# Graph network kernel: ranks counted by partition, uneven transfers issued in two, and the second convolution's table built inside the first convolution's loop

## The chip, the cores and the metric

The kernel runs on one NeuronCore of a Trainium2 chip. The metric is the device time of one execution, in microseconds (us). The core has five engines with an instruction stream each: TensorE (PE, matrix products, with weight loads shown as PEld), VectorE (DVE), ScalarE (ACT), GpSimd (POOL) and SyncE (SP, which here only issues transfers). Transfers between HBM and the on-chip memory (SBUF) are issued by SP, ACT or POOL, each from its own instruction stream, and are done by 16 DMA engines. Matrix products land in PSUM, which has eight banks.

## The reference: what is computed

A graph of N = 6250 nodes with 128 features each and E = 100000 edges, sorted by destination. Two layers, each followed by a layer norm over the features:

```python
edge_index = stack([src, dst])
x = layernorm(x + sigmoid(gcn(relu(gcn(x, W1, b1)), W2, b2)))      # layer 0: two graph convolutions
x = layernorm(x + attention(x, edge_attr, fc_w, fc_r_w, attn_w, loop_w, src, dst))   # layer 1

# one graph convolution; a loop of weight 1 is added to every node
deg  = segment_sum(ew, dst)
dinv = rsqrt(deg)
out  = segment_sum((x @ W)[src] * (dinv[src] * ew * dinv[dst])[:, None], dst) + b
# layer 1: scores from z[src], z[dst] and the edge attributes, a softmax over the edges of
# each destination, and a sum of alpha * (z[src] + edge_attr @ fc_r_w.T) by destination
```

All is float32. The edge attributes are E x 128 floats, 51 MB, and are read twice.

## The kernel before, in words

**Chunks.** The edges are cut into NC = 49 chunks of 2048 (16 per partition); the last chunk has 1696, so 106 partitions of 16. The edges being sorted by destination, a chunk's destinations lie in a window of WC = 144 consecutive nodes whose start is read at run time (`cbase_of`). Nodes are cut into NB = 49 blocks of 128; the last block has 106 nodes.

**Sorting (L688 to L787).** In each chunk the edges are ordered by the block of their source. For every edge the kernel finds its rank, the number of earlier edges of its chunk with the same source block. A comparison makes a one-hot tile `oh` of 128 partitions x 48 blocks x 16 edges (L698). VectorE adds it up over 2, 4 and 8 edges (L703 to L705), and ten TensorE products (L710 to L714) fill a tile of two PSUM banks with, for each edge position and block, the number of earlier edges. ScalarE copies that tile out (L717), and VectorE multiplies it with `oh` and adds it up over the blocks (L718 to L723). When all chunks of a batch (seven, at first three and four) have ranks, each edge gets a slot: 12 groups of 128 slots, in which each quarter takes edges of one source block, and GS = 5 groups for edges that spill. Further one-hot tiles and products move each edge's source row, window position and weight to its slot (L757 to L773). The source rows of a batch go to HBM (`srd`, L781).

**One convolution (`pick`, `weigh`, `scatter`, `add_in`, L467 to L527).** The table, one row for each node, lies in HBM (`g1`, `g2`) and, its first 48 blocks split into three bf16 parts, in SBUF (`hot`). For a chunk, `pick` multiplies a mask of the slots (a comparison of the slot's source row with the partition, L853) with `hot` on TensorE (144 products, L476); ScalarE copies the result out with the edge weights (L481); POOL gathers the spilled edges' rows from HBM (L485); VectorE makes the window positions one-hot (L491, L498). `scatter` sums the 17 groups into the window on TensorE (L522), `add_in` adds the window to the accumulator on VectorE (L527).

**The stages.** Preparation and the node degrees (to about 115 us). The table of the first convolution (`table_of`, L324): for each four blocks four products with W1, a scaled copy, a store to `g1`, the split into `hot`, and a transpose into the accumulator `acc1`, which so starts with the node's own term. The first convolution's loop (L862), in which the sorting of the later chunks is interleaved: it is done when seven chunks are left. Then all of `acc1` is scaled by dinv (L308) and goes through bias and ReLU (L885), and `table_of` builds the second table from it, into `g2`, `hot` and a second accumulator `acc2`. The second convolution's loop (L999) loads the masks back from HBM, and in it VectorE also multiplies the edge attributes by the attention vector and adds them up (L980, L981); in steps of four blocks, nodes that are done go on to the first layer's result and the table of the second layer (`x1_of` under `Pieces`: `go` takes up a group of blocks once the running window has passed it). That table goes to HBM (`zd`, and split in `hz`); the attention stage (L1028 on) loads `hot` again from `hz` in four slices on ACT's queue (L1191), computes the scores (L1053 to L1097) and the softmax in batches, and runs the last loop.

**What sets the order.** Each engine runs its instructions in program order. The order is fixed at build time by a planner that goes through the program with a cost model and takes what is ready, in the order of the program where several are; it inserts the semaphore waits and gives tiles a place as their buffers come free. The second convolution's loop is kept as written (`manual_schedule`). The first convolution's loop is not. A pool's `bufs` says how many buffers a tile has in turn.

**Lines of the prediction's steps.** L308 scaling by dinv, L320 to L322 the split of a table (its last subtraction on POOL), L423 to L425 the same split in `x1_of`, L333 and L340 products and transposes of `table_of`, L334 and L342 ScalarE's copies in it, L421 to L426 the parts' store, L827 the load of the degrees, L849 and L854 the load of slot rows and the store of masks, L994 the load of edge attributes, L1106 the load of one batch's scores.

## Time and profile before

| | |
|---|---|
| median of 8 executions | 1987.57 us (1983.59 to 1993.39) |
| the profiled execution | 1987.97 us; its span, first to last instruction, 1986.2 us |
| mean granted TensorE clock in it | 0.90 of full speed |
| TensorE / VectorE / ScalarE / POOL busy | 80% / 82% / 48% / 56% of the span |
| first convolution's loop | about 170 to 678 us |
| second table | about 678 to 735 us |
| second convolution's loop | about 735 to 1194 us |
| attention stage | about 1194 to 1986 us |
| moved by DMA | 307 MB, 155 GB/s over the span |

In the profile L12 is line 12 of the kernel before; an arrow `out<-in` names the tile written and those read. In a list in order of time a line gives the start, the duration, the engine and the operation, and in square brackets how long the engine sat idle before it and what ended that. `DMA_DIRECT2D` on SPq or ACTq is the issue of a transfer, not its duration. In a list of waits the columns are the total, the number of times and the longest, in us.

### The profile page before, as it was taken

Reading aid. Unit: us, or ns where it says so; the run is one execution under the profiler, and the core shown is the slowest. Engines: PE = TensorE matmul, PEld = TensorE weight load, DVE = VectorE, ACT = ScalarE, POOL = GpSimd, SP = SyncE. Lnnn points to the kernel's source line nnn. Section 1 sums busy time; section 2 is a strip of 40 time slices with the busy share of each in tenths; the row PEclk is TensorE's granted clock in tenths of the full one; section 3 lists DMA queues with packets and bytes.
Section 4 is the critical chain, followed back from the end, with each engine's and each line's share of the span. In section 5 each row is a group of like instructions: output and inputs, shape, how many; then the busy total and the mean of one; then the engine's idle time right before and its main releaser. Section 6 shows DMA issues by size and latency. Waiting matters only on the chain.

```text
span 1986.2 us, 78720 instructions
## 1 busy us (share of the span) xinstructions
PE 1591.2 (80%) x33767; PEld 1439.9 (72%) x33767; DVE 1633.0 (82%) x3252; ACT 945.8 (48%) x3098; POOL 1107.1 (56%) x953
## 2 busy tenths in 40 slices
PE   2867889989987868888888884568888888888996
PEld 2556878878877757778778872457777777877985
DVE  7788978888977338998989965889989898997773
ACT  1255445455455655667667663113343343434543
POOL 4025766676676548888888860215344343434762
PEclk9978989999988959899989995569899999999998
DMA  2114244244245337777767774636656666655662
GB/s 63 37 44 151 68 117 132 48 144 138 64 124 179 76 120 222 236 228 226 253 219 237 243 230 131 180 106 173 181 159 191 169 179 179 180 165 144 191 184 68
DMA packets 254593, 306.90 MB, mean 155 GB/s; under 512 B 37857, under 2 KB 193255, under 8 KB 247182
## 3 DMA queue, kind: packets, MB, share of 16 engines
q1 hardware_dynamic: 222627, 244.90, 39.1%
q0 software_dynamic: 23520, 48.22, 11.8%
q10 hardware_dynamic: 8088, 8.65, 1.4%
q8 instruction: 268, 4.39, 0.9%
q14 instruction: 90, 0.74, 0.1%
HBM read 260.42 MB, written 41.25 MB: 152 GB/s over the span
## 4 chain that ended last, share of the span: by engine, by line
PE 38%; DVE 35%; DMA 13%; issue 7%; ACT 5%; POOL 1%; DVEq 1%; SPq 0%; ACTq 0%; POOLq 0%
PE win L522 16%; PE g L476 8%; DVE wm L491 5%; DMA far<-g,sidx 4%; DVE sel L1096 3%; DVE put L764 3%; DVE ohm L759 2%; PE rec L1209 2%; DMA rk<-srow 2%; DMA mask<-srd 2%; DMA mask<-masks 2%; PE mm L333 1%; PE k L1093 1%; ACT got L481 1%; PE r L1239 1%
## 5 line engine op out<-in xcount | busy, mean ns | idle before, releaser
L485 POOL DMA_INDIRECT far<-g,sidx x490 | 728.3, 1486 | 231.2 <-PE win L522 94.6
L481 ACT ACTIVATE got<-g,swt 128x128 f32<-128x128 f32 x1764 | 485.9, 381 | 390.2 <-PE g L476 188.1
L485 POOL DMA_INDIRECT far<-zd,sidx x245 | 314.1, 1282 | 451.2 <-PE win L522 330.5
L522 PE MATMUL win<-wm,got 128*128 128x144 f32 x3528 | 524.1, 306 | 11.8 <-issue 11.7
L522 PEld LDWEIGHTS win<-wm,got 128*128 128x128 f32 x3528 | 487.0, 204 | 30.2 <-issue 20.8
L476 PE MATMUL g<-hot,mask 128*32 128x128 bf16 x21168 | 395.2, 230 | 84.7 <-issue 61.4
L476 PEld LDWEIGHTS <-mask 128*32 128x32 bf16 x21168 | 338.8, 102 | 118.9 <-issue 89.6
L491 DVE TENSOR_TENSOR wm<-iota,sdst 128x1728 f32<-128x1728 f32 x147 | 286.8, 1951 | 4.5 <-DMA g<-rows 4.3
L515 ACT ACTIVATE wm<-wm,swt 128x64 f32<-128x64 f32 (+1 forms) x735 | 201.1, 355 | 78.2 <-DVE wm L498 46.4
L522 PE MATMUL win<-wm,far 128*128 128x64 f32 (+1 forms) x1470 | 187.6, 272 | 24.6 <-DMA far<-g,sidx 22.3
L522 PEld LDWEIGHTS win<-wm,far 128*128 128x128 f32 x1470 | 181.9, 194 | 26.6 <-issue 21.4
L527 DVE TENSOR_TENSOR acc<-acc,win 128x144 f32 x147 | 44.4, 302 | 104.2 <-PE win L522 92.1
L1093 PE MATMUL k<-adp,rk 128*128 128x49 bf16 x2352 | 90.6, 193 | 48.9 <-DVE sel L1096 35.3
L980 DVE TENSOR_TENSOR et<-et,ar_row 128x2048 f32<-128x2048 f32 (+1 forms) x49 | 111.6, 2278 | 20.1 <-DMA et<-in_edge_attr_dram 20.1
L1093 PEld LDWEIGHTS <-rk 128*128 128x128 bf16 x2352 | 83.0, 102 | 60.3 <-issue 30.8
L981 DVE TENSOR_REDUCE dots<-et 128x16 f32<-128x2048 f32 (+1 forms) x49 | 112.0, 2286 | 1.7
L322 POOL TENSOR_TENSOR hot<-low,hot 128x512 bf16<-128x512 f32 x24 | 32.5, 1356 | 138.5 <-DVE hot L321 99.2
L1096 DVE TENSOR_TENSOR sel<-k,ohb 128x392 f32<-128x392 f32 x98 | 83.7, 854 | 2.6 <-PE k L1093 2.0
L764 DVE TENSOR_TENSOR put<-ohg,rec 128x1360 bf16<-128x1360 bf16 x49 | 76.9, 1569 | 0.0
L717 ACT CAST own<-r 128x768 bf16<-128x768 f32 x49 | 39.3, 801 | 71.4 <-PE r L714 49.8
L771 PE MATMUL rec<-put,ohm 128*128 128x90 bf16 x784 | 59.7, 244 | 14.8 <-DVE put L767 12.7
L771 PEld LDWEIGHTS <-ohm 128*128 128x128 bf16 x784 | 55.5, 165 | 20.8 <-DVE put L767 10.2
(397 smaller groups left out, 2308.8 us busy)
## 6 DMA issues: line engine op xcount, KB each, us to landing
et<-in_edge_attr_dram SPq DMA_DIRECT2D x97, 512.0 KB
et<-in_edge_attr_dram SPq DMA_DIRECT2D x48, 1024.0 KB
mask<-masks SPq DMA_DIRECT2D x98, 384.0 KB
rk<-srow SPq DMA_DIRECT2D x98, 256.0 KB
mask<-srd SPq DMA_DIRECT2D x49, 384.0 KB
masks<-mask SPq DMA_DIRECT2D x49, 384.0 KB
far<-g,sidx POOLq DMA_INDIRECT x490
g<-rows SPq DMA_DIRECT2D x24, 256.0 KB
```

Of the source, the lines that this page charges most:

```text
L476: nc.tensor.matmul(ps[32 * q : 32 * q + 32, g, :], mask[:, (g0 + g) * P + 32 * q : (g0 + g) * P + 32 * q + 32], hot[:, 4 * (g0 + g) + q, k ...
L481: nc.scalar.activation(got[:, g, :], ps[:, g, :], AF.Copy, scale=swt[:, c, g0 + g : g0 + g + 1])
L485: nc.gpsimd.indirect_dma_start(out=got, out_offset=None, in_=table[:, :], in_offset=bass.IndirectOffsetOnAxis(ap=sidx[:, c, g : g + 1], ax ...
L491: nc.vector.tensor_tensor(wm[:, : GP * WC].rearrange("p (g w) -> p g w", w=WC), iota[:, None, 1 : WC + 1].to_broadcast([P, GP, WC]), sdst[ ...
L515: nc.scalar.activation(m, m, AF.Copy, scale=swt[:, c, g : g + 1])
L522: nc.tensor.matmul(ps[:, n0 : n0 + m.shape[-1]], rows[g], m, start=g == 0, stop=g == G - 1)
L764: nc.vector.tensor_tensor(put[:, :, : G * F].rearrange("p t (g f) -> p t g f", f=F), ohg[:, :, :, None].to_broadcast([P, TC, G, F]), rec[: ...
L771: nc.tensor.matmul(ps, ohm[:, :, t], put[:, t, :], start=t == 0, stop=t == TC - 1)
L980: nc.vector.tensor_mul(et[:n], et[:n], ar_row[:n, None, :].to_broadcast([n, TC, D]))
L981: nc.vector.tensor_reduce(dots[:n, c, :], et[:n], AX.X, OP.add)
L1093: nc.tensor.matmul(ps[:, s, :], mk[:, s * P : (s + 1) * P], adp[:, 0, k, :NB], start=k == 0, stop=k == 2)
L1096: nc.vector.tensor_mul(sel, ps, ohb.rearrange("p b s -> p s b"))
```

## The change

Four edits, in one step.

1. *Ranks by partition.* The rank of an edge may count the edges of its chunk in any fixed order. Now the partitions are ordered by a spread number (partition x 79 mod 128, `first`), and inside a partition the order of the 16 edges holds. The edges of earlier partitions are counted by sixteen TensorE products of 48 columns that add up in one tile of one PSUM bank, of which there are two; ScalarE copies that tile out, repeated 16 times. The edges of the same partition are counted on VectorE: a 16 x 16 comparison of the source blocks, a product with a lower triangle, a reduction into `near`, which is added once a batch. The additions L703 to L705 and the ten products L710 to L714 go.
2. *Uneven transfers in two.* `even(n)` cuts a transfer over n partitions into one over the largest multiple of 16 and one over the rest. It is used for the last block of nodes (106: 96 and 10), the last chunk's edge attributes (106), the degrees (49: 48 and 1) and the scores of a batch (34, 82 or 114).
3. *The second table in the first loop.* `h_of` takes a group of four blocks of `acc1`, once the window has passed it, through scaling, bias, ReLU, the product with W2, the store to `g2`, the transpose back into `acc1` and the split into three bf16 parts, which go to HBM (`hh`). Two steps of it are called in each turn of the loop; what is left runs after the loop. `hot` is then loaded from `hh` in four slices on ACT's queue. The tile of the rows (`hrows`) and that of the parts (`hpart`) have one buffer, and the first subtraction of the split writes in place into `hrows`. To make room in PSUM the window tile of this loop has one bank in place of two.
4. *One tile for both sums.* `acc2` is `acc1`.

```diff
+    spread = const.tile([P, P + 1], I32, name="spread")
+    for of, at in ((iota_i[:, :P], slice(0, P)), (iotap_i[:, 0:1], slice(P, P + 1))):
+        nc.vector.tensor_scalar(spread[:, at], of, 79, None, op0=OP.mult)
+        nc.vector.tensor_scalar(spread[:, at], spread[:, at], P - 1, None, op0=OP.bitwise_and)
+    spread_f = const.tile([P, P + 1], F32, name="spread_f")
+    nc.vector.tensor_copy(spread_f, spread)
+    first = const.tile([P, P], BF16, name="first")
+    nc.vector.tensor_scalar(first, spread_f[:, :P], spread_f[:, P:], None, op0=OP.is_gt)
+    lower = const.tile([P, TC, TC], BF16, name="lower")
+    nc.vector.tensor_tensor(lower, iotab[:, None, :TC].to_broadcast([P, TC, TC]),
+                            iotab[:, :TC, None].to_broadcast([P, TC, TC]), op=OP.is_lt)
...
+    def even(n):
+        cut = n // 16 * 16
+        return [slice(a, b) for a, b in ((0, cut), (cut, n)) if b > a]
...
         if b1_ == NB:
-            eng.dma_start(table[(NB - 1) * P : N, :], of[:tail, NB - 1 - b0, :])
+            for r in even(tail):
+                eng.dma_start(table[(NB - 1) * P + r.start : (NB - 1) * P + r.stop, :], of[r, NB - 1 - b0, :])
...
+    def h_of(acc, b0, n, xp, pool):
+        some = blocks[b0 : b0 + n]
+        w = sum(nb for _, nb in some)
+        at = slice(b0 * P, b0 * P + w)
+        scale = by_dinv(acc, b0, n, xp)
+        next(scale)
+        yield
+        next(scale, None)
+        yield
+        nc.scalar.activation(acc[:, at], acc[:, at], AF.Relu, bias=cols[:, 0:1])
+        yield
+        st = xp.tile([P, 4, D], F32, name="hrows", bufs=1)
+        ps = pool.tile([P, 4, D], F32, name="mm")
+        for b, nb in some:
+            nc.tensor.matmul(ps[:nb, b - b0, :], acc[:, b * P : b * P + nb], w2, start=True, stop=True)
+            nc.scalar.activation(st[:nb, b - b0, :], ps[:nb, b - b0, :], AF.Copy, scale=dinv[:nb, b : b + 1])
+        store_blocks(nc.sync, g2, st, b0, n)
+        yield
+        ps = pool.tile([P, 512], F32, name="mm")
+        for b, nb in some:
+            nc.tensor.transpose(ps[:, (b - b0) * P : (b - b0) * P + nb], st[:nb, b - b0, :], ident[:nb, :nb])
+        nc.scalar.copy(acc[:, at], ps[:, :w])
+        if b0 < BP:
+            m = min(n, BP - b0)
+            part = xp.tile([P, 4, 3, D], BF16, name="hpart", bufs=1)
+            nc.scalar.copy(part[:, :m, 0, :], st[:, :m])
+            yield
+            left = st[:, :m]
+            nc.vector.tensor_sub(left, left, part[:, :m, 0, :])
+            nc.vector.tensor_copy(part[:, :m, 1, :], left)
+            nc.vector.tensor_sub(part[:, :m, 2, :], left, part[:, :m, 1, :])
+            nc.sync.dma_start(hh[:, b0 : b0 + m], part[:, :m])
...
-    ps_r = sorting.enter_context(tc.tile_pool(name="ps_r", bufs=1, space=PSUM))
+    ps_r = sorting.enter_context(tc.tile_pool(name="ps_r", bufs=2, space=PSUM))
...
-                a2 = sp.tile([P, BP, 8], BF16, name="a2")
-                a4 = sp.tile([P, BP, 4], BF16, name="a4")
-                a8 = sp.tile([P, BP, 1], BF16, name="a8")
-                nc.vector.tensor_tensor(a2, oh[:, :, 0:8], oh[:, :, 8:16], op=OP.add)
-                nc.vector.tensor_tensor(a4, a2[:, :, 0:4], a2[:, :, 4:8], op=OP.add)
-                nc.vector.tensor_tensor(a8, a4[:, :, 0:1], a4[:, :, 2:3], op=OP.add)
-                ps = ps_r.tile([P, 2, 512], F32, name="r")
-                for h in range(2):
-                    ks = slice(h * HB, h * HB + HB)
-                    full = ps[:, h, : HB * TC].rearrange("p (k t) -> p k t", t=TC)
-                    nc.tensor.matmul(full, trib, oh[:, ks, :], start=True, stop=False)
-                    nc.tensor.matmul(full[:, :, 8:16], onesb, oh[:, ks, 0:8], start=False, stop=False)
-                    for of, m, w in ((a2, 2, 4), (a4, 4, 2), (a8, 8, 1)):
-                        to = full.rearrange("p k (b i) -> p k b i", b=m)[:, :, :, w : 2 * w]
-                        nc.tensor.matmul(to, onesb, of[:, ks, None, 0:w].to_broadcast([P, HB, m, w]),
-                                         start=False, stop=w == 1)
+                ps = ps_r.tile([P, BP], F32, name="r")
+                for t in range(TC):
+                    nc.tensor.matmul(ps, first, oh[:, :, t], start=t == 0, stop=t == TC - 1)
+                pairs = sp.tile([P, TC, TC], BF16, name="pairs", bufs=1)
+                nc.vector.tensor_tensor(pairs, blk[:, c, :, None].to_broadcast([P, TC, TC]),
+                                        blk[:, c, None, :].to_broadcast([P, TC, TC]), op=OP.is_equal)
+                nc.vector.tensor_mul(pairs, pairs, lower)
+                nc.vector.tensor_reduce(near[:, c - c0, :], pairs, AX.X, OP.add)
                 own = sp.tile([P, BP, TC], BF16, name="own", bufs=2)
-                nc.scalar.copy(own.rearrange("p (h k) t -> p h (k t)", h=2), ps[:, :, : HB * TC])
+                nc.scalar.copy(own, ps[:, :, None].to_broadcast([P, BP, TC]))
...
+            nc.vector.tensor_add(r_, r_, near[:, :n])
...
-            ps_w = ... tile_pool(name="ps_w", bufs=2, space=PSUM)
+            ps_w = ... tile_pool(name="ps_w", bufs=1, space=PSUM), ps_m = ... tile_pool(name="ps_m", bufs=1, space=PSUM)
...
+        pieces = Pieces(lambda b0, n: h_of(acc1, b0, n, hp, ps_m))
...
             if win is not None:
                 add_in(acc1, c - 2, win)
+            pieces.go(lows[max(c - 1, 0)], 1)
             new = pick(c, mask, hot, g1, ps_g, wp, 6, 12)
             sort_to(to)
+            pieces.go(lows[max(c - 1, 0)], 1)
             slot_rows(c + 2)
...
         add_in(acc1, NC - 1, scatter(held, ps_w))
+        pieces.go(N, 999)
+        for b0 in range(0, BP, GP):
+            nc.scalar.dma_start(hot[:, b0 : b0 + GP], hh[:, b0 : b0 + GP])
...
-    with tc.tile_pool(name="rows1", bufs=4) as xp:
-        scaled(acc1, xp)
-    for c, n in chunks512:
-        nc.scalar.activation(acc1[:, c : c + n], acc1[:, c : c + n], AF.Relu, bias=cols[:, 0:1])
-    leftB = ctx.enter_context(ExitStack())
-    acc2 = leftB.enter_context(tc.tile_pool(name="accp2", bufs=1)).tile([P, NP], F32, name="acc2")
-    with tc.tile_pool(name="tab2", bufs=2) as wp, tc.tile_pool(name="ps_t", bufs=3, space=PSUM) as ps_mm:
-        table_of(acc1, w2, g2, hot, acc2, ps_mm, wp)
+    acc2 = acc1
...
-                nc.sync.dma_start(ets[c][:n], ea[c * CC : c * CC + n * TC, :].rearrange("(p t) f -> p t f", t=TC))
+                of = ea[c * CC : c * CC + n * TC, :].rearrange("(p t) f -> p t f", t=TC)
+                for r in even(n):
+                    nc.sync.dma_start(ets[c][r], of[r])
```

The loads of a last block (`load_some`), of the degrees (L827) and of the scores (L1106) are cut by `even` in the same way.

More of the change, by code (lines that the diff above doesn't have):

```diff
@@ L76, in gnn_kernel @@
     BP = 4 * GP
-    HB = BP // 2
     G = GP + GS
@@ L109, in gnn_kernel @@
     hz = dram.tile([P, BP, 3, D], BF16, name="hz")
+    hh = dram.tile([P, BP, 3, D], BF16, name="hh")
     dinvd = dram.tile([NB, P], F32, name="dinvd")
@@ L264, in load_some @@
         if b0 + n >= NB:
-            eng.dma_start(to[:tail, NB - 1 - b0, :], of[(NB - 1) * P : N, :])
+            for r in even(tail):
+                eng.dma_start(to[r, NB - 1 - b0, :], of[(NB - 1) * P + r.start : (NB - 1) * P + r.stop, :])
     def transpose_blocks(pool, to, of, first=0, count=NB):
@@ L692, in sort @@
             some = slice(c0, c0 + n)
+            near = sp.tile([P, BATCH, TC], F32, name="near", bufs=1)
             rank = sp.tile([P, BATCH, TC], F32, name="rank")
@@ L826, in gnn_kernel @@
             degr = xp.tile([NB, 3, P], F32, name="degr")
-            nc.sync.dma_start(degr, degd.rearrange("k b p -> b k p"))
+            for r in even(NB):
+                nc.sync.dma_start(degr[r], degd.rearrange("k b p -> b k p")[r])
             nc.vector.tensor_add(degr[:, 0, :], degr[:, 0, :], degr[:, 1, :])
@@ L837, in gnn_kernel @@
         table_of(xT, w1, g1, hot, acc1, ps_mm, xp, lambda: sort_to(min(done[0] + 1, steps_to(sorts[1][0]))))
-    with tc.tile_pool(name="conv", bufs=2) as wp, tc.tile_pool(name="ps_g", bufs=3, space=PSUM) as ps_g, \
-            tc.tile_pool(name="ps_w", bufs=2, space=PSUM) as ps_w:
+    with tc.tile_pool(name="conv", bufs=2) as wp, tc.tile_pool(name="hp", bufs=2) as hp, \
+            tc.tile_pool(name="ps_g", bufs=3, space=PSUM) as ps_g, \
+            tc.tile_pool(name="ps_w", bufs=1, space=PSUM) as ps_w, tc.tile_pool(name="ps_m", bufs=1, space=PSUM) as ps_m:
         rows_in = {}
@@ L879, in gnn_kernel @@
         add_in(acc1, NC - 1, scatter(held, ps_w))
+        pieces.go(N, 999)
+        for b0 in range(0, BP, GP):
+            nc.scalar.dma_start(hot[:, b0 : b0 + GP], hh[:, b0 : b0 + GP])
     sorting.close()
     edges.close()
-    with tc.tile_pool(name="rows1", bufs=4) as xp:
-        scaled(acc1, xp)
-    for c, n in chunks512:
-        nc.scalar.activation(acc1[:, c : c + n], acc1[:, c : c + n], AF.Relu, bias=cols[:, 0:1])
-    leftB = ctx.enter_context(ExitStack())
-    acc2 = leftB.enter_context(tc.tile_pool(name="accp2", bufs=1)).tile([P, NP], F32, name="acc2")
-    with tc.tile_pool(name="tab2", bufs=2) as wp, tc.tile_pool(name="ps_t", bufs=3, space=PSUM) as ps_mm:
-        table_of(acc1, w2, g2, hot, acc2, ps_mm, wp)
-    rightA.close()
+    acc2 = acc1
     with tc.tile_pool(name="conv2", bufs=2) as wp, tc.tile_pool(name="arp", bufs=2) as ap_, \
@@ L1105, in softmax @@
             ad = lp.tile([P, P], F32, name="ad", bufs=1)
-            nc.sync.dma_start(ad[:R, :], adgd[c0 * CC : c0 * CC + R * P].rearrange("(r j) -> r j", j=P))
+            rows = adgd[c0 * CC : c0 * CC + R * P].rearrange("(r j) -> r j", j=P)
+            for r in even(R):
+                nc.sync.dma_start(ad[r, :], rows[r, :])
             ps = ps_c.tile([P, P], F32, name="rec")
@@ L1290, in gnn_kernel @@
     right_r.close()
-    leftB.close()
+    rightA.close()
     hotp.close()
```

## The prediction

> **What bounds the kernel now.** First the page's shares and slices, to see whether one engine bounds the whole.
>
> ```profile
> PE 1591.2 (80%) x33767; PEld 1439.9 (72%) x33767; DVE 1633.0 (82%) x3252; ACT 945.8 (48%) x3098; POOL 1107.1 (56%) x953
> DVE  7788978888977338998989965889989898997773
> ```
>
> VectorE and TensorE share the lead, but the two 3s in VectorE's slices (680 to 740 us) are a stage in which neither works much. So the stages come next, as stretches of the first convolution's loop and what follows it (columns: stretch, length, busy time of PE, PEld, DVE, ACT, POOL, granted clock, DMA share, GB/s).
>
> ```profile
> 320.00:400.00 80.00, 70.99 (x1492) 64.69 (x1494) 70.71 (x157) 41.34 (x143) 56.09 (x38) 0.94 0.40 116
> 400.00:480.00 80.00, 69.13 (x1640) 62.08 (x1632) 73.34 (x161) 44.20 (x152) 56.26 (x41) 0.98 0.45 130
> 640.00:680.00 40.00, 37.01 (x804) 35.61 (x804) 17.14 (x29) 25.58 (x88) 23.51 (x20) 0.96 0.44 105
> 680.00:740.00 60.00, 41.44 (x314) 30.49 (x317) 18.12 (x28) 31.93 (x85) 20.10 (x16) 0.60 0.33 107
> ```
>
> While edges are sorted, VectorE is busy 88 to 92% and bounds the loop; after the last sort (from about 625 us) TensorE does. 680:740 is the second table, a chain of TensorE and ScalarE at a clock of 0.60. Then the waits of the loop, 170 to 640 us (us in total, times, longest):
>
> ```profile
> DVE own L718 <- ACT own L717: 20.0, 13, 2.9
> DVE mask L853 <- DMA mask<-srd: 17.0, 11, 6.6
> ...
> SPq L781 <- DVE srT L780: 248.9, 6, 44.8
> ```
>
> VectorE was busy 400 of these 470 us. The third line matters later: SyncE's queue stands still for half of the loop, behind a store that waits for the end of each sorted batch. Last, in order of time, the two edges between loops.
>
> ```profile
> 678.46 0.30 DVE L527 TENSOR_TENSOR acc<-acc,win 128x144 f32 x1 [4.59 <-PE win L522]
> 732.46 0.42 SPq L994 DMA_DIRECT2D et<-in_edge_attr_dram  x1
> 735.44 5.27 PE L476 MATMUL g<-hot,mask 128*32 128x128 bf16 x197 [7.59 <-DMA mask<-masks]
> 737.67 2.29 DVE L980 TENSOR_TENSOR et<-et,ar_row 128x2048 f32<-128x2048 f32 x1 [3.13 <-DMA et<-in_edge_attr_dram]
> 744.66 4.42 PE L522 MATMUL win<-wm,got 128*128 128x144 f32 x24
> ...
> 1165.34 0.26 SPq L994 DMA_DIRECT2D et<-in_edge_attr_dram  x1
> 1196.83 2.29 DVE L980 TENSOR_TENSOR et<-et,ar_row 106x2048 f32<-106x2048 f32 x1 [16.93 <-DMA et<-in_edge_attr_dram]
> 1233.53 0.32 SPq L426 DMA_DIRECT2D hz<-part  x1
> 1236.19 0.33 ACTq L1191 DMA_DIRECT2D hot<-hz  x1
> 1247.56 1.15 PE L476 MATMUL g<-hot,mask 128*32 128x128 bf16 x36
> ```
>
> From the last addition of the first convolution to the first window sum of the second, 678.5 to 744.7, 66 us pass. At the second edge VectorE idles 16.9 us for one load: 848 KB in 106 partitions, 31.5 us from issue to use, where the 1 MB load of 128 partitions at 732.46 took 5.2.
>
> **The ranks.** Per chunk three additions go (L703, L704, L705: 353, 253 and 201 ns in the loop, 807 in all) and three operations come. The comparison of 128x256 resembles L761 (272 elements, one operand repeated innermost, 438 ns): 415. The product of 256 packed bf16 lies between L704 (192, 253) and L703 (384, 353): 286. The reduction of 256 resembles L1097 (392 elements, 555 ns) by length: 416. Sum 1117, so +0.31 us a chunk on VectorE; 42 chunks are sorted in the loop, 13 us, and six batch additions at 270 ns (L742) make 1.6. TensorE's ten matmuls of 192 to 384 columns take 1.2 us a chunk (403.01 to 404.2); sixteen of 48 columns resemble L1209 (51 columns, sixteen in 1.12 us): 0. The moving operand now has a stride of 32 bytes, which no row shows for a moving operand; as weights such a stride loads in 165 ns (L771) against 102 (L1093), so at most +1 us a chunk on TensorE, in the phase where VectorE binds: taken as 0. ScalarE's copy keeps 768 elements (801 ns): 0. Two rank banks in place of one take away part of the 20.0 us that VectorE waits for that copy.
>
> **The second table's work, moved into the loop.** Per piece of four blocks VectorE gets the scaling (L308, 687 ns), two subtractions (L423 681, L425 696, the second one formerly on POOL as L322, 1356 ns) and a cast (L321, 456): 2.52 us. Nine pieces lie in the sorting part: 22.7 us. ScalarE gets 0.735 + 4 x 0.369 + 0.586 + 0.699 = 3.5 us a piece, in a loop where it is busy 52%: hidden by that slack; without it 9 x 3.5 = 31. TensorE: 49 blocks took 41.4 us at a clock of 0.60, so about 2 us a piece at full clock; nine are 18 us, in its 60 idle us of this stretch: hidden while VectorE binds. SyncE carries per piece one row load, one g2 store and now one store to hh (0.35 us of issue each), between the mask stores. VectorE's sum is 13 + 1.6 + 22.7 = 37, less 0.08 us overlap of back-to-back instructions (two of L698 in 1.01 us at 0.55 each), 35. Bounds for the loop: 0 (all of it goes into the 70 us of idle time) and 35/0.88 = 40. I take 26: 35 less about half of the 20 us on the copy, the wait that the second bank bears on.
>
> **The wait added.** The first subtraction writes in place into the tile that the g2 store reads, so VectorE waits for that store; behind it stand masks and sort work, and TensorE's next pick. A store-to-load step takes 2.66 us (1233.53 to 1236.19). From 0 (half a chunk, 5 us, lies between) to 9 x (2.66 + 4.31, a mask-store pair at 412.12 on SyncE) = 63. The nearest row is the mask load, late 11 times in 48 by 1.5 us: 2 or 3 waits of 2 us, +5. The window bank is single now: scatter waits for the addition before it, which starts 0.2 us after its window ends (416.28), 4 us ahead of the next scatter; when it falls behind L491 and L498, 2.4 us, in the seven unsorted chunks 17: +1.
>
> **Edge 1.** Gone are 66 us. New: the last chunk's gathers meet three 1152 KB slices of hot, as those at 1182.84 did (10.63 us in the chain against 4.89 at 673.02): +5. After the last addition, the last piece: scaling 0.40, ReLU 0.49, TensorE 0.7, copies 0.75, store landed 2.66, VectorE 0.8, hh landed 2.66 (rows of the piece at 1224 to 1236): 8.5. Then the fourth slice; its like was used 11.4 us after issue behind other work, and 5.2 us is a free 1 MB load: 8. The rest of pick 0 and pick 1: 3. Together 24.5, gain 42. Ends: -50 (no contention, 5 us slice) and -24 (all 4.6 MB and two 1 MB loads only after the last piece: 6.6 MB at the 240 GB/s of 1000 to 1100 us is 28, with 8.5 and 5, 42). Between, because slices at 1177.64 to 1185.94 went out as the last pick freed them. The piece before shares the single tiles, but starts 5 us earlier (673.56): 0. POOL's gathers wait for g2's last store, 3 us before hh's: 0. On ScalarE's queue the fourth load waits for hh; behind it stand the evictions of pick 0, which need that slice anyway: 0.
>
> **Uneven transfers.** If the 848 KB land like the 1 MB load, VectorE's 16.9 us go, but the second loop's last gathers (10.63) and the rk load behind them (8.09) are late next, still beside the hot slices. 0 to -17; I take -7, half of both. The other splits (1 KB to 53 KB) cost an issue of 0.3 us each; the one wait seen is 0.71 us, the ad load of 3.37 stands once in the chain: -1 (ends -4, +1; the row sum of the degrees used 10 us after issue was not waited for).
>
> [...]
>
> **Before the loop.** Seven chunks at 0.31 us: +2 (ends 0, +5 with the new constants, 1.7 us, whose cover is a 2.59 us wait at 6.5 us).
>
> **Sum.** The profiled execution took 1987.97 us (span 1986.2, 1.8 around it), 0.4 above the median of eight, 1987.57. 26 + 5 + 1 - 42 - 7 - 1 + 2 = -16: 1972.
>
> **Rivals.** *The in-place wait decides (slower).* Place: the subtraction behind g2's store. For: SyncE blocked up to 44.8 us at a time. Against: a store that is ready earlier is queued earlier. Full price 63 instead of 5: 2030; slower begins where each of nine pieces waits 2.8 us (16 + 4 + 5 over 9). *The loop swallows the work.* For: 70 us idle, the second rank bank. Against: 10.00 busy in 10 us at 370:390 and 440:460. Loop 0 and edge -48: 1940. *Reload late.* ScalarE issues all slices after the last piece; edge -24: 1990. For: they come last in the program. Against: the second edge's slices. *Uneven loads hidden anyway.* Edge 2 gives 0: 1979. *The change doesn't do what it says:* pieces pile up at the loop's end, 13 in turn through single buffers at 5.8 us (8.5 less the 2.66 of hh) are 75 us; with hh, slice and picks 89 in place of 66, but only 9 of loop growth: 9 + 6 + 23 - 7 - 1 + 2 = +32, 2020. Against: L308 ran at 639 us, ahead of its place.
>
> **How the numbers follow.** Forecast 0.48, wait 0.15, swallowed 0.15, reload late 0.10, uneven 0.07, piled up 0.05. The forecast's own range is 1956 to 1988. The range of all, 1938 to 2008, takes in the middle of the swallowed case, reload, uneven, and the wait up to 41 of its 63 us; it leaves out the pile, the far end of the wait and the swallowed case's best, some 0.17. A measurement of this kernel tells about 0.2%, 4 us. Faster: 0.43 of the forecast, 0.15, 0.05 of uneven, none else: 0.63. Same: 0.11 (forecast's edge 0.03, reload 0.05, uneven 0.02, wait 0.01). The rest, 0.26, is slower.
>
> **What would show it.** Right: the three additions gone, 1.1 us of new VectorE work a chunk; the sorting part 20 to 35 us longer with VectorE above 90%; the last addition to the first window sum of the second loop in 22 to 30 us; the 106-partition load used without a wait, its loop's end 5 to 10 us nearer. Wrong: VectorE waiting for DMA at a subtraction, a loop no longer than before, slices of hot issued only after the last piece, or gathers that stay at 10 us at the second edge.

## The result: slower by 0.9%, and the profile after

| | before | after |
|---|---|---|
| median of the compared runs | 1987.04 us | 2006.67 us |
| ratio, with its 95% interval | | 1.0091 (1.0071 to 1.0111), some 18 us |
| profiled execution: span, granted clock | 1986.2 us, 0.900 | 2014.0 us, 0.891 |

The forecast was 1972, 16 us faster. The ratio is that of the means of the fast runs, 2005.0 and 1987.0 us; two runs of after, at 2021.45 and 2023.71 us over 1.5% above its fastest (1989.97), count as slow and are left out. The profiled execution of after, 2015.89 us, is 9 us above the median of its kind. Its 27.8 us over before are located by the additions of windows to the sum, one for each chunk and loop, whose starts the timeline gives (us):

| | last addition of loop 1 | first of loop 2 | last of all | end of the span |
|---|---|---|---|---|
| before | 678.5 | 752.3 | 1966.7 | 1986.2 |
| after | 732.5 | 771.8 | 1984.4 | 2014.0 |
| growth of the stretch that ends there | +54.0 | -34.5 | -1.8 | +10.1 |

The column sums make 27.8. Three things are not as forecast: the stretch to the end of the first loop grew by 54 and not by 34 (26 + 5 + 1 + 2), the first edge gave 34.5 and not 42, and the last 20 us of the kernel, which the prediction does not mention at all, took 10 us more. The second edge gave nothing. Of the 54 us, 7.6 come ahead of the first addition (188.8 to 196.3 us, at a granted clock of 0.74 from 120 to 190 us against 0.83 before; the forecast had 2), 43.7 between the first addition and the 42nd.

First the loop while edges are sorted, from the first window addition to the 42nd, as one stretch (columns: stretch, length, busy time of PE, PEld, DVE, ACT, POOL, granted clock, DMA share, GB/s), before and after.

```profile
189.00:617.00 428.00, 377.98 (x8212) 348.02 (x8210) 375.92 (x798) 218.68 (x761) 297.91 (x200) 0.94 0.36 102
```

```profile
196.00:668.00 472.00, 417.69 (x8545) 392.36 (x8544) 402.37 (x838) 246.25 (x827) 290.38 (x200) 0.92 0.37 109
```

Before, VectorE was busy for 88% of it, and so was TensorE: the two are level, and I had read the one and not the other. After, TensorE is still at 88%, VectorE at 85%. VectorE's busy time grew by 26.5 us, its idle time by 17.5 (52.1 to 69.6), and TensorE's busy time by 39.7. So the 44 us of this stretch are not VectorE's work alone. Of TensorE's 39.7, the two parts measured alone, further down, show 22.6 (14.5 in e11, 8.1 in e10). The granted clock is 0.92 here, against 0.94 before, 0.93 in e10 and 0.96 in e11; whether it makes the rest is not shown. Its largest waits in it, after (us in total, times, longest):

```profile
DVE acc L583 <- PE win L578: 24.8, 17, 3.1
DVE own L767 <- ACT own L766: 13.3, 12, 3.2
DVE sr L826 <- ACT slots L822: 9.3, 4, 3.6
DVE mask L905 <- DMA mask<-srd: 7.8, 7, 2.0
DVE hrows L397 <- PE mm L389: 4.6, 2, 3.2
```

In the same stretch before, the waits for a window were 13.7 and those for slot rows 3.7; those for the ranks' copy were 20.0 and are 13.3. VectorE waits longer for TensorE, and TensorE waits 7.8 us for additions to free the single window bank, a wait that the stretch before does not have. The wait for the store to g2, which the change adds by writing in place, is 6.2 us in the whole loop, and 4.7 of that at its end.

The first edge, in order of time (start, duration, engine, line, operation; in brackets idle time before and what ended it):

```profile
732.50 0.30 DVE L583 TENSOR_TENSOR acc<-acc,win 128x144 f32 x1 [5.26 <-PE win L578]
...
732.86 0.53 SPq L1046 DMA_DIRECT2D et<-in_edge_attr_dram  x1
...
734.94 0.40 DVE L329 TENSOR_TENSOR acc<-acc,dr 128x234 f32<-128x234 f32 x1
...
738.15 1.69 PE L532 MATMUL g<-hot,mask 128*32 128x128 bf16 x56 [5.38 <-issue]
...
739.77 0.80 PE L383 MATMUL mm<-w,acc 128*128 128x128 f32 x2
...
740.54 2.29 DVE L1030 TENSOR_TENSOR et<-et,ar_row 128x2048 f32<-128x2048 f32 x1 [4.81 <-DMA et<-in_edge_attr_dram]
...
742.39 0.51 ACT L394 CAST hpart<-hrows 128x384 bf16<-128x384 f32 x1
...
746.94 0.55 DVE L397 TENSOR_TENSOR hrows<-hrows,hpart 128x384 f32<-128x384 f32 x1
...
748.28 2.28 DVE L1030 TENSOR_TENSOR et<-et,ar_row 128x2048 f32<-128x2048 f32 x1
...
754.97 0.34 SPq L400 DMA_DIRECT2D hh<-hpart  x1
...
756.62 0.33 ACTq L938 DMA_DIRECT2D hot<-hh  x1
...
767.20 3.06 PE L578 MATMUL win<-wm,got 128*128 128x144 f32 x20
```

After the last scaling (734.94) the last blocks' parts should have landed 8 us later. Their store was issued at 754.97, because both engines that they need had the second loop's first work in front. TensorE stood 5.38 us at that loop's first pick, while slices of `hot` were still loading, with the blocks' products queued behind it: three of the four slices were issued from 720.47 to 727.27, and from 732.5 to 738.1 1.12 MB still came in on their queue. VectorE stood 4.81 us for edge attributes, and did two multiplications, two reductions and one-hot windows before and between the short steps of the split.

At the second edge the 106-partition load is now used without a wait, as forecast. But the chain there goes through the last gathers (start, duration):

```profile
1204.45 2.28 DVE L1030 TENSOR_TENSOR et<-et,ar_row 106x2048 f32<-106x2048 f32 x1
```

```profile
1184.20 6.12 DMA far<-g,sidx
...
1190.68 8.05 DMA far<-g,sidx
...
1209.11 7.89 DMA far<-g,sidx
```

Last, the kernel's end, before and after: the last store of the output, the first step of a closing test of the slots on VectorE, and its last.

```profile
1968.00 0.48 DVE L1303 TENSOR_TENSOR off<-sdst,fpart 128x240 f32<-128x240 bf16 x2 [1.02 <-PE agg L438]
...
1971.24 0.14 DVE L1315 CAST slow_r<-any__43481 1x1 int32<-1x1 f32 x1
...
1975.30 0.27 SPq L231 DMA_DIRECT2D out_dram<-fin  x1
```

```profile
1992.19 0.73 SPq L251 DMA_DIRECT2D out_dram<-fin  x2
...
1994.28 0.48 DVE L1357 TENSOR_TENSOR off<-sdst,fpart 128x240 f32<-128x240 bf16 x2 [3.23 <-DMA out_dram<-fin]
...
1997.52 0.14 DVE L1369 CAST slow_r<-any__43736 1x1 int32<-1x1 f32 x1
```

Before, the test ran beside the last load of `x1d`, 4 us ahead of the last store. After, its first step waits until the last store has landed, and the kernel ends 16.5 us after its last step (before, 15.0 after). Edit 4 is the likely cause: `acc2` lay on the left side of SBUF and was freed there just before the test's tiles were placed; now it is `acc1`, on the right side. That the test's tiles came to lie over those of the output, which the stores still read, is argued from this and from the waits (in the rows above the first step waits for the last product that reads the sum, `agg`, before, and for the store of `fin` after); the profile shows no addresses, and no run has edit 3 without edit 4.

### The profile page after: what moved, and what is told of

It is laid out like the page before. It is cut to its first block, busy times and chain, and to the rows that moved or that the text cites. A ratio compares the mean times of both kernels' runs of the same rounds, so it can differ in the third digit from the quotient of the medians.

```text
span 2014.0 us, 79261 instructions
## 1 busy us (share of the span) xinstructions
PE 1606.9 (80%) x34061; PEld 1475.4 (73%) x34061; DVE 1651.8 (82%) x3281; ACT 945.0 (47%) x3099; POOL 1074.7 (53%) x941
## 4 chain that ended last, share of the span: by engine, by line
PE 44%; DVE 32%; DMA 9%; issue 7%; ACT 4%; POOL 1%; DVEq 1%; SPq 0%; ACTq 0%; POOLq 0%
PE win L578 20%; PE g L532 9%; DVE wm L547 4%; PE r L758 3%; DVE sel L1148 3%; DVE et L1030 2%; PE rec L1263 2%; DVE put L814 2%; PE rec L821 2%; DMA rk<-srow 1%; PE k L1145 1%; ACT got L537 1%; DVE ohm L809 1%; DMA mask<-srd 1%; DMA far<-g,sidx 1%
## 5 line engine op out<-in xcount | busy, mean ns | idle before, releaser
L541 POOL DMA_INDIRECT far<-g,sidx x490 | 714.2, 1458 | 324.5 <-PE win L578 164.4
L578 PE MATMUL win<-wm,got 128*128 128x144 f32 x3528 | 537.9, 311 | 21.9 <-issue 13.5
L541 POOL DMA_INDIRECT far<-zd,sidx x245 | 305.1, 1245 | 452.7 <-PE win L578 350.3
L578 PEld LDWEIGHTS win<-wm,got 128*128 128x128 f32 x3528 | 499.8, 209 | 41.2 <-issue 22.3
L758 PE MATMUL r<-oh,first 128*128 128x48 bf16 x784 | 79.0, 267 | 13.2 <-DVE oh L754 11.1
L758 PEld LDWEIGHTS <-first 128*128 128x128 bf16 x784 | 68.8, 118 | 18.2 <-DVE oh L754 8.7
```

The source lines that it names most:

```text
L541: nc.gpsimd.indirect_dma_start(out=got, out_offset=None, in_=table[:, :], in_offset=bass.IndirectOffsetOnAxis(ap=sidx[:, c, g : g + 1], ax ...
L578: nc.tensor.matmul(ps[:, n0 : n0 + m.shape[-1]], rows[g], m, start=g == 0, stop=g == G - 1)
L758: nc.tensor.matmul(ps, first, oh[:, :, t], start=t == 0, stop=t == TC - 1)
```

## The experiments

The runs fell on several chips, and ratios are always against the kernel before on the same chip. On two of them before took 1987.2 and 1986.25 us, like the 1987.04 above. On the others it took 2353 to 2404, at a mean granted clock of 0.83 to 0.86 in place of 0.90. I call those throttled. There VectorE is busy only 65% while edges are sorted (150 of 230 us, 170 to 400 us of e1). TensorE is busy for 183 of these 230 us and stands for 39 more in pauses that nothing in the record explains (5 us in the same stretch before), so TensorE sets the time, and these chips answer other questions.

**The parts alone, on a throttled chip.** Theory: VectorE's work sets the loop, as forecast. Rival: TensorE does.

e1 is the kernel before with `even` alone, e2 with the new ranks alone, e3 with edits 3 and 4 alone (the diffs are the parts of the change). 

> The kernel before with the uneven transfers in two and nothing else. The forecast's term for this part was -8 us (second edge -7, the other splits -1): 0.996 of before. Rival, from the chain of waits before: it runs through the last gathered rows (10.63 us) and the load behind them and not through the 106-partition load, so VectorE's 16.9 us of idle time there cost nothing: 0, within 4 us of before. Both expect VectorE to use the 106-partition load without a wait.

> The kernel before with the new ranks alone (sixteen products of 48 columns, the count inside a partition on VectorE, two rank banks). VectorE theory: 13 + 1.6 us in the loop and 2 before it, less 10 for the wait that the second bank bears on: +7, at most +17. TensorE theory: in the kernel after, sixteen products take 1.43 to 1.52 us against 1.2 before, so 42 x 0.25 to 0.3 = 11 to 13 us more on TensorE as well, where both engines take turns on the chain: +15 to +30.

> The kernel before with the second table's work in the first loop and one tile for both sums, old ranks, transfers uncut. The forecast's terms for this part: loop +21, store wait +5, window bank +1, first edge -42: -15, so 1972. TensorE theory: the trace after shows per piece four products in turn with four copies (0.50 + 0.42 us each) on the chain and a first edge of about 36 us in place of 66: loop +30 to +40, edge -30, so 0 to +10.

Measured: e1 1.0033 (0.9995 to 1.0071), e2 1.0061 (1.0028 to 1.0094), e3 0.9933 (0.9899 to 0.9966). VectorE used the 106-partition load without a wait, and the time gained nothing. The ranks cost 15 us (7 to 23), which fits either theory, and the second table gains 16 us (8 to 24) here, where TensorE binds and its work is only moved. That this is the forecast's -15 is luck: on a chip at 1987 us the sign turns (e11, below).

e4 is the kernel after with this edit:

```diff
         for b, nb in some:
             nc.tensor.matmul(ps[:nb, b - b0, :], acc[:, b * P : b * P + nb], w2, start=True, stop=True)
+        for b, nb in some:
             nc.scalar.activation(st[:nb, b - b0, :], ps[:nb, b - b0, :], AF.Copy, scale=dinv[:nb, b : b + 1])
```

> The kernel after, with the four products of a piece issued first and their four scaled copies behind them, in place of product, copy, product, copy. If TensorE's stand between the products (0.42 us, three times a piece, thirteen pieces) lies on the path: 11 to 16 us faster than after, about 1993. If VectorE binds the loop and TensorE's stand is covered: no change, 2007 within 4.

Measured: 0.9967 (0.9930 to 1.0004), to be read beside e7, which ran on another throttled chip.

**The same beside the kernel after, and the grouped products on the table alone.** All four ran on a second throttled chip.

> The kernel before with the new ranks alone, once more, beside the kernel after. VectorE theory (0.31 us a chunk, less the wait for the copy): +7, at most +17, ratio 1.004. TensorE theory (sixteen products of 1.43 to 1.52 us against 1.2, twenty weight loads at 118 ns): +15 to +30, ratio 1.008 to 1.015.

> The kernel before with the second table's work in the first loop alone, once more, beside the kernel after. Forecast: -15 (ratio 0.992). TensorE theory: 0 to +10 (1.000 to 1.005), the loss of after then coming half from here.

> The kernel after as it is, on the chip of the two parts. If the parts add up, its ratio less 1 is the sum of the parts' ratios less 1 and of the uneven transfers' (0.000 to 0.003). If the parts meet (both want VectorE and TensorE in the sorting part), it is above that sum by more than 0.004.

> The second table's work in the first loop alone, with the four products of a piece issued first and the four scaled copies behind them. If TensorE's stand between the products lies on the path: 11 to 16 us under the version that takes product and copy in turn (ratio lower by 0.005 to 0.008). If it is covered: the same within 0.002.

Measured: ranks 1.0045 (1.0017 to 1.0072), table 0.9946 (0.9911 to 0.9981), after 1.0031 (0.9998 to 1.0064), table with grouped products 0.9845 (0.9791 to 0.9898, five runs). The parts add up: 0.45 - 0.54 + 0.33 from e1 is 0.24%, against 0.31. The grouped products are 1.0% under the table alone, 24 us, and the intervals are apart; e4 is 0.6% under e7, 15 us, on another chip and with intervals that overlap at their ends. On these chips TensorE's stand between product and copy lies on the path.

**The tail.** e9 has the table alone with grouped products, and three edits at the loop's end: pieces after the last pick write their parts into `hot`, the slices stored by then are loaded before them, and the second loop is ordered behind the last piece on VectorE and TensorE.

```diff
-            part = xp.tile([P, 4, 3, D], BF16, name="hpart", bufs=1)
+            if late:
+                part = hot[:, b0 : b0 + m]
+            else:
+                part = xp.tile([P, 4, 3, D], BF16, name="hpart", bufs=1)
+                via.append((b0, m))
...
+        late.append(1)
...
+        for b0 in range(0, end, GP):
+            b1 = min(b0 + GP, end)
+            nc.scalar.dma_start(hot[:, b0:b1], hh[:, b0:b1])
         pieces.go(N, 999)
...
-        with tc.manual_schedule():
+        with tc.issue_after(behind_h[0]), tc.issue_after(behind_h[1]), tc.manual_schedule():
```

> The second table's work in the first loop with old ranks and uncut transfers; the products of a piece issued first; and the tail of the first edge changed: what is still to do after the last pick writes its three parts straight into hot (no store to hh and no load back), the slices already stored are loaded before it, and the second loop's first work on VectorE and TensorE is ordered behind the last piece. In the trace of after the last piece's VectorE steps stand behind the second loop's first edge-attribute multiplications and a load they wait for (734.9 to 750.6 us for 2 us of work), then 1.63 and 5.62 us of store and load. If that order is what the first edge lost: last addition to first window sum 20 to 24 us in place of 35 to 40, so 12 to 18 us under the version without these edits (about 0.980 of before where that one gave 0.9845). If the reload of the other slices or the masks come late anyway: within 4 us of it.

Measured, on a chip at 1987 us: 1.0012 (0.9981 to 1.0044), not 0.980. The comparison with 0.9845 was void, since that was a throttled chip's. The order was as wanted, but a wait of the change took the place (chain, start and duration):

```profile
698.08 9.99 DMA far<-g,sidx
...
708.78 1.48 PE mm L365 x6
...
711.20 10.22 DMA g<-hrows
...
721.54 0.57 DVE hrows L385
```

VectorE's first subtraction, in place in `hrows`, waited 10.22 us for the 192 KB store of those rows, which was issued on SyncE's queue behind two loads of masks and two 1 MB loads of edge attributes, all issued in the 2.4 us before it. That queue moved 2.97 MB in these 10 us, the queue of the slices of `hot` 0.10. That is the prediction's first rival, at one place.

**The parts alone at 1987 us, and the tail without its waits.** e10 and e11 repeat the two parts. e12 is e9 without three waits:

```diff
             left = st[:, :m]
+            if (b0, m) not in via:
+                left = xp.tile([P, 512], F32, name="dr")[:, : m * D].rearrange("p (b f) -> p b f", f=D)
-            nc.vector.tensor_sub(left, left, part[:, :m, 0, :])
+            nc.vector.tensor_sub(left, st[:, :m], part[:, :m, 0, :])
...
+        if n > 2:
+            st = xp.tile([P, 4, D], F32, name="hrows", bufs=1)
+        else:
+            st = xp.tile([P, 6, D], F32, name="hlast", tag="hpart", bufs=1)
...
-                next(rows_of, None)
+                if c > 1:
+                    next(rows_of, None)
```

> The kernel before with the new ranks alone, wanted on a chip where before takes 1987 us. VectorE theory: +7, at most +17 (ratio 1.004 to 1.0085), the loop 7 to 15 us longer. TensorE theory (1.43 to 1.52 us of products a chunk against 1.2, weights loaded again for each of the sixteen, chunk by chunk on the chain): the loop 20 to 26 us longer, ratio 1.010 to 1.013; that is what is left of the 54 us of after when the 30 us of the version with the table alone and a changed tail are taken off.

> The kernel before with the second table's work in the first loop alone, wanted on a chip where before takes 1987 us. Forecast: loop +27, edge -42, together -15 (ratio 0.992). By the traces since: loop +30, first edge -34 as in after, second edge 0: -4, ratio 0.998, and then most of the 18 us of after come from the ranks. If the two parts meet in the loop instead, this one and the ranks alone are both under 0.2% and their sum is far from after.

> The version with the table alone and the changed tail, with three waits of its tail taken away: after the last pick the subtraction goes to a tile of its own (the load of dinv's tile, free by then) and the last rows to another, so that neither waits for a store of rows, and the row work of the second loop starts two chunks later, so that its loads of dst don't stand before the next masks. In the trace of the version without these, VectorE waited 10.22 us for the store of rows at 711 us, and the masks came 4.3 us late at 743 us behind loads of dst. If that was what the first edge lost: first window addition of the second loop 8 to 14 us earlier, ratio 0.994 to 0.997. If the reload of hot is late anyway: no change, 1.001.

e10 to e12 were measured on one chip, e9 on another. The growth of each stretch of the profiled execution is over the profile of before shown above (the four terms make the difference of the spans):

| | ratio (95%) | to the last addition of loop 1 | first edge | second loop and attention | end |
|---|---|---|---|---|---|
| e10, ranks | 1.0042 (1.0019 to 1.0066) | +5.6 | -0.3 | -1.7 | 0.0 |
| e11, table | 1.0077 (1.0043 to 1.0112) | +36.0 | -34.4 | -11.3 | +10.2 |
| e9, changed tail | 1.0012 (0.9981 to 1.0044) | +30.3 | -32.6 | +3.9 | +10.7 |
| e12, tail without waits | 0.9967 (0.9939 to 0.9994) | +31.1 | -45.2 | -2.2 | +10.9 |

The ranks cost 8 us (4 to 13); the VectorE theory's +7 holds for the time, the TensorE theory's 20 to 26 us of loop does not; the 5.6 us are under the VectorE theory's 7 to 15 as well, and 3.2 of them come ahead of the first window addition. The table costs 15 us (9 to 22), where -15 was forecast and -4 expected by the traces since. Its profiled execution is the quickest of its ten and owes that to the -11.3; +36.0 - 34.4 + 10.2 is +12, within the interval. The two medians make 23.6, after is at 18 (14 to 22): no sign that the parts hinder each other. The +12 of loop that the profile of after has over the two parts is about the 9 us by which that execution is above its median.

In e10 the new work on VectorE is of the size forecast (columns: line, engine, operation, tiles; busy time, mean ns; idle time before):

```profile
L718 DVE TENSOR_TENSOR pairs<-blk 128x256 bf16<-128x256 bf16 x39 | 16.3, 419 | 0.2
L721 DVE TENSOR_REDUCE near<-pairs 128x16 f32<-128x256 bf16 x39 | 16.0, 411 | 0.0
...
L720 DVE TENSOR_TENSOR pairs<-pairs,lower 128x256 bf16<-128x256 bf16 x39 | 11.0, 282 | 0.1
```

But the second rank bank did not shorten the wait for the copy, 20.0 before:

```profile
DVE own L724 <- ACT own L723: 20.8, 19, 2.5
```

The sorting part as a stretch, first window addition to 42nd, in e11 and in e12:

```profile
191.00:652.00 461.00, 392.50 (x8200) 355.48 (x8200) 394.81 (x835) 243.13 (x822) 295.38 (x198) 0.96 0.39 113
```

```profile
194.00:646.00 452.00, 386.36 (x8167) 356.04 (x8167) 395.12 (x835) 241.32 (x823) 267.28 (x197) 0.94 0.40 115
```

In both VectorE is busy 19 us more than before; it idles 14 us more in e11 (windows +6.0, slot rows +6.1, the store to g2 5.5) and 5 us more in e12. The difference of the two, 9 us, goes with grouped products (e9's stretch is 456 us long). Where product and copy go in turn, TensorE waits for the copies; this row of the products of a piece, in the same stretch of e11, gives what it waited for, the total in us and the number of times:

```profile
  ACT hrows L364: 9.5, 28
```

In e9 and e12 the same products do not wait for a copy in that stretch. By time e9 is 13 us under e11, on another chip, with a first edge that is no shorter. The single window bank makes little here: TensorE's wait for an addition before a window is 1.6 us in e11 and 1.4 in e12.

In e12 the last piece goes through without a stop: last addition 709.57, last step of the split 716.13, first window sum 724.41 (timeline):

```profile
709.57 0.31 DVE L577 TENSOR_TENSOR acc<-acc,win 128x144 f32 x1 [8.48 <-PE win L572]
...
716.13 0.29 DVE L392 TENSOR_TENSOR hot<-dr,hot 128x128 bf16<-128x128 f32 x1
...
724.41 3.21 PE L572 MATMUL win<-wm,got 128*128 128x144 f32 x24
...
737.13 1.08 PE L572 MATMUL win<-wm,far 128*128 128x64 f32 x4 [2.50 <-DMA far<-g,sidx]
```

That is 14.8 us in place of 66.2 before and 34.7 after. After that the first window waits for its gathers, 737.13. Its addition comes 11.7 us earlier than in e9, as expected. e12 is the only version measured under before at 1987 us, by 6.6 us (1.2 to 12.1). It still has the 10.9 us at the end; an estimate without them is 17 us under before, which was not run.

**What makes the loop's idle time.** Three versions of e12: e13 and e17 issue a piece's two stores from ScalarE's and POOL's queues, e14 and e18 let windows and pieces share two PSUM banks, e15 has one subtraction of each earlier piece on POOL. e16 is e1 again.

```diff
-        store_blocks(nc.sync, g2, st, b0, n)
+        store_blocks(nc.scalar, g2, st, b0, n)
...
-                nc.sync.dma_start(hh[:, b0 : b0 + m], part[:, :m])
+                nc.gpsimd.dma_start(hh[:, b0 : b0 + m], part[:, :m])
```

```diff
-            tc.tile_pool(name="ps_w", bufs=1, space=PSUM) as ps_w, tc.tile_pool(name="ps_m", bufs=1, space=PSUM) as ps_m:
+            tc.tile_pool(name="ps_w", bufs=2, space=PSUM) as ps_w:
...
-        ps = pool.tile([P, 4, D], F32, name="mm")
+        ps = pool.tile([P, 4, D], F32, name="mm", tag="win")
```

```diff
-            behind_h[1] = nc.vector.tensor_sub(part[:, :m, 2, :], left, part[:, :m, 1, :]).ins
+            eng = nc.gpsimd if (b0, m) in via else nc.vector
+            behind_h[1] = eng.tensor_sub(part[:, :m, 2, :], left, part[:, :m, 1, :]).ins
```

> The version with the changed tail, with the two stores of a piece issued from other queues: the rows to g2 from ScalarE, which makes them, the parts to hh from POOL. In the trace of the table alone SyncE's queue stood 86.4 us before stores of parts (10 times, longest 22.4) and 60.1 us before stores of rows, and VectorE waited 26.3 us for loaded slot rows in place of 17.0. If SyncE's queue makes the loop's idle time: loop 8 to 15 us shorter than the tail version's (chunk 48 added at about 696 in place of 709.6), ratio 0.990 to 0.993. If not: the same, 0.9967, or slower where the issue costs POOL and ScalarE more than it frees.

> The version with the changed tail, with the window's and the pieces' tiles sharing two PSUM banks in place of one bank each, so that a window has its second bank back except while a piece is in TensorE. The forecast gave the single bank +1 us, at most +17. If it is +1: no change (0.9967). If the single bank is what made the loop longer (VectorE waited 39.3 us for windows with the table alone against 32.9, TensorE 8.3 us for additions in after): 6 to 16 us faster, 0.989 to 0.993.

> The version with the changed tail, with the last subtraction of every piece before the tail on POOL (1.36 us there, 0.69 on VectorE), 11 pieces. If VectorE's work sets the loop, as forecast: 7.6 us less on it, 6 to 7 us faster (0.993). If waits set it: no change (0.9967), or slower where POOL's gathers come later.

> The kernel before with the uneven transfers in two and nothing else, on a chip at 1987 us. Forecast: -8 us (0.996). Rival: the chain at the second edge runs through the last gathered rows and the load behind them: 0 (0.998 to 1.002), with the 106-partition load used without a wait.

> The version with the changed tail and a piece's two stores on ScalarE's and POOL's queues, once more, wanted at 1987 us. If SyncE's queue makes the loop's new idle time: chunk 48 added 8 to 15 us earlier than in the tail version (709.6), ratio 0.990 to 0.993. If not, as the throttled chip had it: the same, 0.9967 within 0.002.

> The version with the changed tail and two PSUM banks shared by windows and pieces, once more, wanted at 1987 us. Forecast (single bank costs +1): no change, 0.9967. If the single bank makes the loop's new idle time: chunk 48 added 6 to 16 us earlier than in the tail version (709.6), ratio 0.989 to 0.993.

All six fell on throttled chips: e13 0.9880 (0.9839 to 0.9921), e14 0.9915 (0.9875 to 0.9954), e15 0.9868 (0.9789 to 0.9947), e16 1.0041 (0.9995 to 1.0088), e17 0.9891 (0.9840 to 0.9942), e18 0.9929 (0.9893 to 0.9966). e12 itself was not run there, and the intervals overlap, so none of the three causes is shown or excluded for 1987 us. In e13 VectorE's wait for slot rows, at least, did not go when the two stores left SyncE's queue (170 to 830 us):

```profile
DVE mask L904 <- DMA mask<-srd: 45.0, 10, 15.6
```

With the stores on SyncE's queue they made, in the same stretch, 38.9 us in e14, 29.2 in e15 and 35.2 in e8, all on throttled chips. e16 agrees with e1: the uneven transfers in two gain nothing on throttled chips (1.0041 and 1.0033).

## Why the prediction was wrong

**What bounds the kernel.** Right that VectorE is busy 88% and more while edges are sorted; wrong that it alone binds there. The same rows show TensorE at 70.99 and 69.13 of 80 us, and the work that went to TensorE was booked at 0. The sorting part grew by 44 us where 20 to 35 were to show, with VectorE at 85% and not above 90%.

**The ranks.** Right in the work of one chunk (1117 ns forecast, 1112 measured for the three operations) and, by luck, in sum: 13 + 1.6 + 2 - 10 is +7, measured 8. The terms in it were not right. The -10 for the copy's wait did not come (20.8 us in e10). VectorE's busy time in the sorting part grew by 5.5 us (375.9 to 381.4) and not by 14.6; that 35 and not 42 chunks have their new operations there explains a part of it. TensorE's 0 was 8.1 us of busy time in the sorting part (378.0 to 386.1): sixteen products took 1.42 to 1.59 us in the chain of after, not the 1.12 of the row that they were held to resemble.

**The second table in the loop.** This is the step that failed: edits 3 and 4 were put at -15 us and cost 15 in e11, 30 of the 34 us by which the forecast missed. Three of their terms were wrong, the loop, the first edge and the kernel's end. In the loop the forecast was 22.7 + 5 + 1, measured 36.0 in e11, and 30.3 and 31.1 where products are grouped. VectorE's 22.7 were about right (+19 busy), the store's wait was 5.5 for 5, and the single window bank 1.6 for 1 in e11 (7.8 in after). The failed term is "TensorE: hidden while VectorE binds": in the order written, three of a piece's four products stand behind a copy of ScalarE (9.5 us of the sorting part in e11, none in e9 and e12), and VectorE waits longer for windows. Undoing that stand took 15 to 24 us off on throttled chips and 5 to 9 us off the sorting part at 1987 us (one profile each). What makes up the rest, SyncE's queue or VectorE itself, stays open.

**Edge 1.** Forecast -42, measured -34.5 (after) and -34.4 (e11); in the forecast's own measure, last addition to first window sum, 34.7 us stood for 24.5. Failed term: the last piece, 8.5. It took 20 us to the issue of its last store, since I followed the piece by its data alone and did not ask what stands ahead of it on VectorE and TensorE. e9 and e12 show it: with the order mended and the two waits for a store gone, the edge gives 45.2. That the slices are loaded beside the last chunks was right for three of the four, but they landed late enough to be part of the 5.38 us at the first pick.

**Edge 2.** Forecast -7, measured about 0 (-1.8 for the second loop and all behind it). Right that the load is used without a wait and that the gathers are late next; wrong to take half. The chain of waits before went through the gathers (10.63 us) and the load of `rk` (8.09) and not through VectorE's 16.9 us. Alone, the split gained no time: 1.0033 and 1.0041, both on throttled chips; at 1987 us it was not run alone. The load itself came sooner: the two parts were issued at 1191.91 and used without a wait at 1204.45, 12.5 us later, where the whole one took 31.5 us and VectorE waited 16.9 for it. No run shows why.

**What was not in the sum.** The end of the kernel, +10. From the last addition to the end of the span all fourteen profiled versions with one tile for both sums take 29.4 to 31.7 us, and all six others 19.3 to 19.5, on every chip. The prediction has no term for edit 4. That it and not edit 3 moves the test is argued above and not shown.

**The rivals.** "Reload late", at 1990, was nearest in kind: slices still loading go with 5.38 us at the first pick, the last piece cost more. "The in-place wait decides" is shown at one place in e9, 10.2 us, and decides nothing in after (6.2 us for the forecast's 5). "The loop swallows the work" did not happen: the loop grew by more than was forecast. "Uneven loads hidden anyway" was right. The pile-up did not happen; pieces kept pace with the windows.

**The sum again**, with what the profile of after has in place of the forecast: 54.0 for 34, -34.5 for -42, -1.8 for -8, and +10.1 for nothing make 27.8 for -16; the median has 18.

## What to carry to other kernels

Here work taken into a loop in which VectorE and TensorE were both busy 88% was not hidden: the second table made the loop 30.3 to 36.0 us longer (e9, e12, e11). So sum the new work on every engine and compare each with that engine's share in the stretch, not with that of the busiest one alone. At an edge between stages follow the last piece through each engine's queue, since a planner may put the next stage's first work, and the loads it waits for, ahead of it; here the ordering, with the last parts written straight into `hot` and the waits for stores taken away, made the edge 10.8 us shorter (45.2 against 34.4), more than the 6.6 us that the best version of the whole move gained. And when a tile changes its place in memory, look at what is placed there next, as far as the kernel's very end (10.1 us here, with that as the likely cause).

## What was not expected of the hardware

The same kernel took 1987 us on two chips and 2353 to 2404 on others, and a change's sign went with it: the table alone 1.0077 there, 0.9933 and 0.9946 here. The granted clock fell only from 0.90 to 0.83 to 0.86, by 4 to 8%, where the time grew by 18 to 21%. Part of the difference shows as pauses in which TensorE waits for nothing in the record, after every four products (e3, chain of waits):

```profile
760.97 0.43 issue
761.40 0.34 PE g L512 x4
761.73 0.43 issue
...
764.01 1.11 issue
765.12 0.32 PE g L512 x4
```

No run here shows what makes these pauses.

A 192 KB store took 10.2 us in e9, behind two loads of masks and two 1 MB loads of edge attributes on the same queue, where the prediction had 2.66 for a store and a load in turn.
